# A four-layer gated transformer on one core: the last layer's expert blocks scatter with addition into the output tensor instead of an internal one

## The chip, the cores and the metric

The kernel runs on one NeuronCore of a Trainium2 chip. The core has five engines with queues of their own: TensorE (PE, with its weight loads listed as PEld), VectorE (DVE), ScalarE (ACT), GpSimd (POOL) and SyncE (SP). Matrix products go to PSUM, everything else lives in SBUF or in HBM. SP and ACT issue plain DMAs; indirect DMAs, whose row numbers come from a table in SBUF, are issued by POOL. All DMAs share 16 DMA engines. The metric is the device time of one execution in microseconds; the median of three runs stands for a kernel, and one further execution was recorded by the hardware profiler.

## The reference

The input x is 4 x 256 tokens of 256 values. Four layers follow, each with a gated cross attention to 64 context tokens and a gated feed-forward part: `x = x + tanh(g) * part(layernorm(x))`. The feed-forward parts are a mixture of 16 experts with 6 chosen for each token (layer 0), a ternary-weight network (layer 1), an int8 linear map (layer 2), and again a mixture of experts (layer 3), the one that matters here, cut to its core:

```python
shared_out = silu_and_mul(x @ shared_gate_up) @ shared_down
probs = softmax(x @ gate_w)
topk_w, topk_i = lax.top_k(probs, K)              # K = 2 of E = 8 experts
topk_w = topk_w / sum(topk_w)
combine = sum(one_hot(topk_i, E) * topk_w[..., None], axis=1)
for e in range(E):
    moe_out += combine[:, e, None] * (silu_and_mul(x @ w_gate_up[e]) @ w_down[e])
return moe_out + shared_out
```

Its result, times the gate and added to x, is the kernel's output, 1024 rows of 256 float32 values, 1 KB each.

## The kernel before

**Tiling.** x is held in SBUF as eight tiles of 128 tokens. Layer 3's feed-forward part is `ffn3` (L1425). It normalises the tokens, stores them with their expert weights in an internal HBM tensor `xd`, and works out the routing; beside this it computes the shared expert tile by tile and adds it to x. `keep_rows` (L369) then stores the eight tiles of x in the internal HBM tensor `sums3` from SP's queue (L372), each as soon as its tile of x is finished. What is left is to add the routed experts' results to those rows.

**Blocks.** The routing sorts the 2048 pairs of token and expert into blocks of 128 slots, each block of one expert. An expert's last block is padded. For every slot there are two tables in SBUF, `gather` and `scatter`, made in `placed` (L1133 to L1138). A padding slot of partition p has the scatter index 1024 + p, so the padding rows of a block land in 128 spare rows at the end of `sums3`, which therefore has T + P = 1152 rows. In the same way layer 0's two tensors `sums0` have spare rows. `prepare` (L303) sets the spare rows of all three tensors to zero early in the kernel, with DMAs of 128 KB from a tile of zeros through `zeroed` (L361, issued at L362).

**The loop over blocks.** `Experts` (L1168) serves layers 0 and 3. For block i, `fetch` (L1183) gathers 128 rows of `xd` with an indirect DMA on POOL, four blocks ahead. `turn` (L1194) transposes them on PE, `up` (L1218) multiplies with the expert's two up matrices in SBUF and applies silu (L1246) and the product with the weight (L1247), `turn_hidden` (L1249) transposes the result, and `down` (L1258) multiplies with the down matrix and copies the product to a slot of a ring of eight (on DVE, L1271, for odd blocks, on ACT, L1273, for even ones). Last, `down` issues the scatter (L1274): an indirect DMA on POOL that adds the 128 rows of the ring's slot to the rows of `sums` that the scatter table names. Two blocks can hold the same token, so each scatter waits on POOL's queue until the one before it on the same tensor has landed. Layer 3 has one such tensor, layer 0 two in turn.

**What is sure to run.** In layer 3 the first 20 blocks (`SURE3`) always run; three more stand behind `tc.If` (L1286), under a test of how many blocks are in use. With the reference's inputs the eight experts get 238, 522, 384, 159, 181, 179, 130 and 255 rows, which make just 20 blocks and leave 512 padding slots in them.

**The end.** After the last step four DMAs copy 256 rows each from `sums3` to the output tensor `out`, HBM to HBM, two from SP and two from ACT (L1670 to L1674). They wait for the last scatter to land. Then comes the closing block, whose instructions the profile puts at L1808: SP passes a row of waits for everything outstanding, each engine drains, and all five meet twice at semaphores, with POOL as the one that collects and releases.

**Order.** Instructions of an engine stand in the order in which the framework's scheduler put them; waits between engines and for DMAs are semaphores that the framework derives from reads and writes of tiles and HBM tensors.

Of the kernel before, what the change touches and what calls it, by code (L numbers as in the profile page):

```python
# [29 lines left out]
F32 = mybir.dt.float32  # L30
# [8 lines left out]
P = 128  # L39
B, S, D = 4, 256, 256  # L40
T = B * S
# [41 lines left out]
def tile_flamingo(ctx: ExitStack, tc: tile.TileContext, a: dict, out: bass.AP):  # L83
    nc = tc.nc
# [3 lines left out]
    dram = ctx.enter_context(tc.tile_pool(name="dram", bufs=1, space=bass.MemoryType.DRAM))  # L88
    psum = ctx.enter_context(tc.tile_pool(name="psum", bufs=2, space=bass.MemoryType.PSUM))

    def ps_mm():
        return psum.tile([P, 512], F32, tag="mm", name="mm", bufs=4)
# [4 lines left out]
    def t4(shape, name, dtype=F32):  # L97
        return sb.tile(shape, dtype, tag="t4", name=name, bufs=6)
# [4 lines left out]
    class Carver:  # L103


        def __init__(self, *regions):
            self.left = list(regions)
# [195 lines left out]
    def prepare():  # L303


        work = t4([P, 1024], "work")
        bd_v = work[:, : B * P].rearrange("p (b l) -> p b l", b=B)
        rot = work[:, B * P : B * (P + DC)].rearrange("p (b d) -> p b d", b=B)
        nc.gpsimd.memset(bd_v, 0.0)
        hd = DC // 2  # L310
        cos_k = ropek[:, 0:1, :].to_broadcast([P, B, DC])
        nc.vector.tensor_tensor(kvr, ctx2, cos_k, ALU.mult)
        for lo, hi in ((0, hd), (hd, 0)):
            sin_k = ropek[:, 1:2, lo : lo + hd].to_broadcast([P, B, hd])
            nc.vector.tensor_tensor(rot[:, :, lo : lo + hd], ctx2[:, :, hi : hi + hd], sin_k, ALU.mult)
        nc.vector.tensor_tensor(kvr, kvr, rot, ALU.add)
        yield
        for j in range(2):
            rows = slice(j * L, (j + 1) * L)
            nc.vector.tensor_copy(bd_v[rows, :, j * DC : (j + 1) * DC], kvr[rows])  # L320
        yield
        ps = ps_mm()
        for b in range(B):
            nc.tensor.transpose(ps[:, b * P : (b + 1) * P], bd_v[:, b, :], ident)
        nc.scalar.copy(bd_k.rearrange("p b l -> p (b l)"), ps)
        yield

        ps = ps_mm()
        for b in range(B):
            nc.tensor.transpose(ps[:DC, b * P : (b + 1) * P], ctx2[:, b, :], ident)  # L330
        nc.scalar.copy(ctxT.rearrange("d b j l -> d (b j l)"), ps[:DC, :])
        yield

        bias_t = sb.tile([P, 512], F32, tag="low", name="bias_t", bufs=1)[:96, : 2 * F0]
        nc.sync.dma_start(out=bias_t, in_=a["L0_b13"])
        nc.vector.tensor_copy(causal16, causal)
        nc.vector.tensor_copy(ident16, ident)
        nc.vector.tensor_copy(shared_is, shared_32)
        nc.vector.memset(ones16, 1.0)
        yield  # L340
        yield
        yield
        nc.vector.tensor_copy(bias_0, bias_t)
        for rows in (slice(32, 64), slice(64, 96), slice(64, 96)):

            nc.vector.tensor_tensor(bias_t[rows], bias_t[rows], bias_0[rows], ALU.subtract)
            nc.vector.tensor_copy(bias_0[rows], bias_t[rows])
            yield
        zeros = t4([P, 1024], "zeros")
        nc.gpsimd.memset(zeros, 0.0)  # L350
        for half in range(2):
            zeroed(sums0[1][half * TH : (half + 1) * TH], zeros)
        for sums in (*sums0, *sums3):
            zeroed(sums[T:], zeros)
        yield


    sums0 = [dram.tile([T + P, D], F32, tag=f"sums0{i}", name=f"sums0{i}") for i in range(2)]
    sums3 = [dram.tile([T + P, D], F32, tag="sums3", name="sums3")]

    def zeroed(rows, zeros):  # L361
        nc.sync.dma_start(out=rows.rearrange("(p r) d -> p (r d)", p=P), in_=zeros[:, : rows.shape[0] * D // P])  # L362
# [299 lines left out]
    def attention0(gate):  # L662
# [76 lines left out]

        wide = None  # L740
        later = prepare()
        last: list = []
        output = fold_output(w_kv0, [lambda: (w_o0, NH, lambda: None)])
# [424 lines left out]
    class Experts:  # L1168


        def __init__(self, route, xd, n, nb, stride, width, chunk, sums, w, bias, hTs, between):
            self.gather, self.scatter, self.expert, self.offset, self.used = route
            self.xd, self.experts, self.nb, self.stride = xd, n, nb, stride
            self.width, self.chunk, self.n = width, chunk, width // chunk
            self.sums, self.w, self.bias, self.hTs = sums, w, bias, hTs
            self.between = between
            self.ring = [sb.tile([P, 4, D], F32, tag="xT", name="ring", bufs=2) for _ in range(2)]
            self.weight: dict = {}
            self.xs: dict = {}
            self.at: dict = {}  # L1180
            self.st: dict = {}
# [76 lines left out]
        def down(self, b):  # L1258
            (st, hT), r = self.st.pop(b), self.at.pop(b) + 4 * self.width
            ps = ps_mm()  # L1260
            for j in range(self.n):
                nc.tensor.matmul(  # L1262
                    ps[:, :D],
                    hT[:, j * P : (j + 1) * P],
                    self.w[: self.chunk, bass.ds(r + j * D, D)],
                    start=(j == 0),
                    stop=(j == self.n - 1),
                )
            y = self.ring[b // 4 % 2][:, b % 4, :]
            if b % 2:  # L1270
                nc.vector.tensor_copy(y, ps[:, :D])  # L1271
            else:
                nc.scalar.copy(y, ps[:, :D])  # L1273
            nc.gpsimd.indirect_dma_start(  # L1274
                out=self.sums[b % len(self.sums)],
                out_offset=bass.IndirectOffsetOnAxis(ap=self.scatter[:, b : b + 1].bitcast(U32), axis=0),
                in_=y,
                in_offset=None,
                compute_op=ALU.add,
            )  # L1280

        def run(self, sure):
# [38 lines left out]
    def ffn0(gate):  # L1321
# [45 lines left out]
        def down(t):  # L1367
# [12 lines left out]
            gated_add(t, ps[:, :D], gate)  # L1380

        in_three(NT, up, turn, down)
        for _ in steps:
            pass
# [40 lines left out]
    def ffn3(gate):  # L1425
# [39 lines left out]
        def down(t):  # L1465
# [4 lines left out]
            gated_add(t, ps[:, :D], gate)  # L1470

        in_three(NT, up, turn, down)
        for _ in steps:
            pass
# [55 lines left out]
    def ffn1(gate):  # L1530
# [45 lines left out]
        def down(g, terms):  # L1576
            for i in range(TPG):
# [12 lines left out]
                gated_add(g * TPG + i, y, gate)  # L1590

        in_turn(NG, up, down)
        used("L1_w1")
        used("L1_w2")
# [72 lines left out]
            kept["weights2"] = weights2(tg[:, 6:7])  # L1667
        step(tg[:, k : k + 1])

    for i in range(4):  # L1670
        rows = slice(i * T // 4, (i + 1) * T // 4)
        to, of = (v[rows].rearrange("(p r) d -> p (r d)", r=4) for v in (out, sums3[0]))
        engine = nc.scalar if i % 2 else nc.sync
        engine.dma_start(out=to, in_=of)  # L1674

def _rope(length, dim):
# [133 lines left out]
```

## Time and profile before

| what | value |
|---|---|
| median of three runs | 948.43 us (945.85 to 948.74) |
| the profiled execution: its time | 947.2 us |
| its span, first to last instruction | 945.4 us |
| mean granted TensorE clock | 0.959 |
| PE busy | 844.9 us (89%) |
| DVE, POOL, ACT busy | 514.0, 344.5, 288.7 us |
| layer 3's 20 scatters | 1573 ns each on POOL, 827.1 to 935.2 us |
| layer 3's 20 gathers | 973 ns each on POOL |
| copies to the output | issued 939.0 to 939.7 us |

The time of an execution is a little longer than its span, here by 1.8 us. An engine's busy time counts its instructions' durations; waits, branches and the issue of DMAs on SP and ACT are not in it. [...]"DMA to landing" is the time from the issue to the completion semaphore. In the tables of groups, a line names source line, engine, operation, what is written and read and how often, then busy time and mean duration, then the idle time of the engine just before and what ended most of it. In lists of one tensor's or one line's instructions the three durations are the smallest, the median and the largest, followed by the first and the last start. In the chain of work, each line has a start, a length and an item of the chain.

### The profile page before, as it was taken

The numbers are of one execution on the slowest core, as the hardware profiler recorded it, in microseconds if no ns is written. First come the engines' busy times: TensorE is split into PE (matmuls) and PEld (weight loads), VectorE is DVE, ScalarE is ACT, GpSimd is POOL, SyncE is SP. The second block draws the span as 40 slices with busy tenths as digits, with TensorE's granted clock in tenths as the row PEclk, the third lists the DMA queues.
The fourth block names the chain that finished last, engine by engine and source line by source line (L and its number), as shares of the span: only waits on it lengthen the run. The fifth ranks groups of instructions, "written<-read, shape, count | busy, mean of one in ns | idle before, by whom it ended". The sixth has DMA issues, their size and how long they took to land. (4 is left out here: it accounts for less than half of the span.)

```text
span 945.4 us, 12712 instructions
## 1 busy us (share of the span) xinstructions
PE 844.9 (89%) x4464; PEld 547.3 (58%) x4467; DVE 514.0 (54%) x1299; ACT 288.7 (31%) x561; POOL 344.5 (36%) x262
## 2 busy tenths in 40 slices
PE   5999999999999998899089997899869899999994
PEld 4544335876667875676045873665545556666662
DVE  4666457756934344573146765778777865222220
ACT  2221004433222332233013436516545531122221
POOL 0455452310066777787201232502312402144321
PEclk9999999999999998999589999989989999999997
DMA  9200228101156555654570000180000011122223
GB/s 359 93 16 22 79 65 258 52 18 32 56 158 161 125 121 128 156 86 71 117 266 1 1 1 1 42 302 2 1 23 1 1 47 58 40 47 48 38 23 66
DMA packets 38762, 75.15 MB, mean 79 GB/s; under 512 B 6240, under 2 KB 26706, under 8 KB 37322
## 3 DMA queue, kind: packets, MB, share of 16 engines
q1 hardware_dynamic: 23562, 52.01, 16.4%
q0 software_dynamic: 14496, 20.47, 12.9%
q10 hardware_dynamic: 640, 1.84, 0.5%
q8 instruction: 39, 0.64, 0.3%
q14 instruction: 25, 0.20, 0.1%
HBM read 58.73 MB, written 16.61 MB: 80 GB/s over the span
## 5 line engine op out<-in xcount | busy, mean ns | idle before, releaser
L438 POOL TENSOR_TENSOR attn<-attn,sm 128x1024 f32<-128x1024 f32 x32 | 60.8, 1901 | 197.1 <-DVE sm L437 163.9
L1247 DVE SCALAR_TENSOR_TENSOR blk<-wide,weight,blk 128x176 f32<-128x176 f32 (+1 forms) x75 | 37.0, 494 | 138.0 <-ACT blk L1246 137.9
L1274 POOL DMA_INDIRECT sums<-ring,big x55 | 87.5, 1590 | 34.9 <-issue 10.8
L422 PE MATMUL wide<-xT,big 128*128 128x512 f32 x192 | 88.3, 610 | 0.3 <-ACT big L557 0.3
L684 DVE TENSOR_TENSOR rope<-wide,big 128x512 f32<-128x512 f32 x96 | 59.6, 684 | 48.8 <-PE wide L422 47.5
L1227 PE MATMUL wide<-big,blk 128*128 x220 | 77.0, 472 | 0.1
L1186 POOL DMA_INDIRECT xs<-xd,big x55 | 55.1, 1001 | 55.8 <-DMA sums<-x 35.6
L1238 PE MATMUL wide<-big,blk 128*128 x160 | 72.2, 593 | 0.5 <-DVE blk L1199 0.5
L1246 ACT ACTIVATE blk<-wide 128x176 f32<-128x176 f32 (+1 forms) x75 | 29.4, 392 | 122.5 <-PE wide L1238 60.2
L422 PEld LDWEIGHTS wide<-xT,big 128*128 128x128 f32 x192 | 35.8, 193 | 47.6 <-issue 41.3
L657 PE MATMUL mm<-vo,attnT 128*128 128x256 f32 x256 | 58.6, 382 | 0.9 <-ACT attnT L453 0.9
L1262 PE MATMUL mm<-big,blk 88*128 x220 | 57.6, 384 | 0.5 <-ACT blk L1255 0.5
L407 PE MATMUL mm<-ident,xn 128*128 128x128 f32 x112 | 19.9, 322 | 41.5 <-DVE xn L395 35.4
L657 PEld LDWEIGHTS mm<-vo,attnT 128*128 128x128 f32 x256 | 47.4, 190 | 8.7 <-ACT attnT L453 2.9
L453 ACT COPY attnT<-mm 128x512 f32<-128x512 f32 x64 | 34.6, 589 | 54.7 <-PE mm L452 54.2
L1262 PEld LDWEIGHTS mm<-big,blk 88*128 88x128 f32 x220 | 42.0, 192 | 16.0 <-ACT blk L1255 1.4
L1227 PEld LDWEIGHTS wide<-big,blk 128*128 128x128 f32 x220 | 40.7, 196 | 13.3 <-issue 1.2
L436 DVE TENSOR_REDUCE sm<-attn 128x16 f32<-128x1024 f32 x32 | 38.8, 1213 | 16.3 <-ACT attn L430 13.7
L1186 POOL DMA_INDIRECT xs<-xd,scratch x20 | 19.5, 973 | 76.2 <-PE mm L1198 54.0
L1274 POOL DMA_INDIRECT sums<-ring,scratch x20 | 31.5, 1573 | 39.2 <-ACT ring L1273 16.8
L1238 PEld LDWEIGHTS wide<-big,blk 128*128 128x128 f32 x160 | 28.8, 190 | 28.9 <-issue 28.2
L407 PEld LDWEIGHTS mm<-ident,xn 128*128 128x128 f32 x112 | 15.1, 162 | 47.2 <-ACT rstd L383 27.6
(321 smaller groups left out, 1704.3 us busy)
## 6 DMA issues: line engine op xcount, KB each, us to landing
big<-in_L_w_gate_up SPq DMA_DIRECT2D x8, 1024.0 KB, 8.2
big<-in_L_w SPq DMA_DIRECT2D x4, 1408.0 KB, 7.9
big<-in_L_w_down SPq DMA_DIRECT2D x8, 512.0 KB, 9.3
w_L_qk<-in_L_qk SPq DMA_DIRECT2D x4, 896.0 KB, 8.7
big<-in_L_w SPq DMA_DIRECT2D x4, 704.0 KB
big<-in_L_wo SPq DMA_DIRECT2D x1, 2048.0 KB, 12.9
xd<-xn SPq DMA_DIRECT2D x16, 128.0 KB, 1.8
sums<-x SPq DMA_DIRECT2D x16, 128.0 KB, 1.8
```

Source lines behind the costliest of these rows:

```text
L407: nc.tensor.transpose(ps[:, i * P : (i + 1) * P], n[:, c * P : (c + 1) * P], ident)
L422: nc.tensor.matmul(ps, w(c), xT[:, c, :], start=(c == 0), stop=(c == 1))
L436: nc.vector.tensor_reduce(sm, e, AX.X, ALU.add)
L438: nc.gpsimd.tensor_tensor(e, e, sm.unsqueeze(2).to_broadcast([P, groups, n]), ALU.mult)
L657: nc.tensor.matmul(ps[:, :D], aT[:, s, :], vo[:, s, :], start=(s == 0), stop=(s == NP - 1))
L684: nc.vector.tensor_tensor(m[:, s, :].rearrange("q (b t) -> q b t", t=S), ps[:, s, :].rearrange("q (b t) -> q b t", t=S), table, ALU.mult,)
L1186: nc.gpsimd.indirect_dma_start(out=xs, out_offset=None, in_=self.xd, in_offset=bass.IndirectOffsetOnAxis(ap=self.gather[:, b : b + 1].bitc ...
L1227: nc.tensor.matmul(ps[:, 0, : 2 * n], st[:, c * P : (c + 1) * P], self.w[:, bass.ds(r + c * 2 * n, 2 * n)], start=False, stop=(c == 1),)
L1238: nc.tensor.matmul(ps[:, k, :n], st[:, c * P : (c + 1) * P], self.w[:, bass.ds(r + (2 * c + k) * n, n)], start=(c == 0), stop=(c == 1),)
L1247: nc.vector.scalar_tensor_tensor(s, lin, self.weight.pop(b), s, ALU.mult, ALU.mult)
L1262: nc.tensor.matmul(ps[:, :D], hT[:, j * P : (j + 1) * P], self.w[: self.chunk, bass.ds(r + j * D, D)], start=(j == 0), stop=(j == self.n - 1),
L1274: nc.gpsimd.indirect_dma_start(out=self.sums[b % len(self.sums)], out_offset=bass.IndirectOffsetOnAxis(ap=self.scatter[:, b : b + 1].bitca ...
```

## The change

Layer 3's sum tensor is now the output tensor itself, so `keep_rows` stores layer 3's x there and the scatters add to it. The output has 1024 rows and no spare ones. The scatters of layer 3 therefore carry a bound, 1023: a row whose index is greater is out of bounds, and that is declared not to be an error. Layer 0's tensors have 1152 rows, so its scatters keep having no bound. The spare rows of layer 3's tensor no longer exist and aren't set to zero. The four copies at the end are gone.

```diff
-        for sums in (*sums0, *sums3):
+        for sums in sums0:
             zeroed(sums[T:], zeros)
         yield
...
     sums0 = [dram.tile([T + P, D], F32, tag=f"sums0{i}", name=f"sums0{i}") for i in range(2)]
-    sums3 = [dram.tile([T + P, D], F32, tag="sums3", name="sums3")]
+    sums3 = [out]
...
             self.between = between
+            rows = sums[0].shape[0]
+            self.bound = rows - 1 if rows == T else None
...
                 in_offset=None,
                 compute_op=ALU.add,
+                bounds_check=self.bound,
+                oob_is_err=self.bound is None,
             )
...
-    for i in range(4):
-        rows = slice(i * T // 4, (i + 1) * T // 4)
-        to, of = (v[rows].rearrange("(p r) d -> p (r d)", r=4) for v in (out, sums3[0]))
-        engine = nc.scalar if i % 2 else nc.sync
-        engine.dma_start(out=to, in_=of)
```

## The prediction

> **What bounds the kernel now.** I read the page's slices first, for where TensorE is the limit and where it is not.
>
> ```profile
> span 945.4 us, 12712 instructions
> PE   5999999999999998899089997899869899999994
> DMA  9200228101156555654570000180000011122223
> ```
>
> Each digit is a fortieth of the span, 23.6 us. TensorE is busy nine tenths nearly everywhere, layer 3's expert blocks included (the last five slices), and only the last slice falls to 4: the tail is where something else sets the end. The table by stage shows both:
>
> ```profile
> 827.00:931.00 104.00, 103.33 (x390) 64.50 (x388) 26.69 (x71) 24.66 (x45) 38.42 (x29) 1.00 0.26 38
> 939.00:945.40 6.40, 0.00 (x0) 0.00 (x0) 0.00 (x0) 0.00 (x0) 0.00 (x0) 0.50 0.48 165
> ```
>
> The columns are length, then busy time (and count) of PE, PE's weight loads, DVE, ACT, POOL. From the first scatter to the last up-projections PE works 103.33 of 104 us; in the last 6.4 us no engine works at all. What is between them, from the chain that ended last:
>
> ```profile
> 928.17 1.74 PE mm L1262 x8
> ...
> 930.76 3.72 DMA sums<-ring,scratch
> ...
> 935.32 1.44 POOL sums L1274
> ```
>
> Block 18's scatter is issued at 930.76 and lands 3.72 us later; only then may block 19's go (935.21, its data had been ready since 933.51). After it come the four copies to the output:
>
> ```profile
> L1674 SPq DMA_DIRECT2D out_dram<-sums x2: 529/548/567, 939.0 to 939.7; - x2
> L1674 ACTq DMA_DIRECT2D out_dram<-sums x2: 598/686/775, 939.0 to 939.7; - x2
> DMA to landing us min/median/max: 3.9/4.2/4.4
> ```
>
> They start at 939.02, so the last scatter landed about 938.96 (935.21 + 3.75). The last two are issued at 939.7 and land 4.4 us or a little more later, about 944.3. Last I asked for the closing block (L1808), where every engine meets:
>
> ```profile
> L1808 SPq EVENT_SEMAPHORE  x14: 17/28/28, 940.3 to 945.3; - x14
> L1808 POOLq EVENT_SEMAPHORE  x4: 17/17/17, 944.6 to 945.3; - x4
> L1808 POOLq DRAIN  x3: 50/109/4327, 936.6 to 945.1; - x3
> ```
>
> SP first passes twelve waits here, then all engines meet at POOL's event of 944.6; from there to the end are 0.8 us. The third line matters: POOL's first drain starts at 936.57 and lasts 4.33 us, to 940.90, which is 1.94 us after the last scatter's landing. Today it is hidden under the copies.
>
> **Part 1, the closing copies go.** Today: landing 938.96, copies until 944.3, closing to 945.4. Without them two paths lead to the meeting point:
> - SP: landing 938.96; its remaining waits are already satisfied and pass at 62 ns each (eight of them between 940.27 and 940.70), at most twelve, so 0.7 us: 939.7.
> - POOL: the drain, to 940.90.
> The later one decides. From the drain: 940.90 + 0.8 = 941.7 us of span, 3.7 us saved. From SP alone: 939.7 + 0.1 + 0.8 = 940.6, 4.8 us saved. Here a rule stands against the row. The Trainium skill, "VectorE: DVE Perf Modes", section "The DRAIN you can't avoid", says that the drains of a kernel's start and end are boilerplate of about 12 ns on all five engines. By it POOL's drain would be free and the saving 4.8 us; by the row it is 4.33 us long. The row decides here: SP's drains do last 7 ns, but this one stands behind a scatter in flight, and it still does after the change. I take 3.7 and keep 4.8 as the other end: if the drain waits for the copies rather than for the scatter, it shrinks.
>
> A second rule bears on the size. "DMA: Bandwidth & Descriptors", "Anatomy of one DMA", puts a software-issued DMA at 2.0 us plus bytes over 436 GB/s. For 1 MB in all that estimates 4.4 us from first issue to last landing; the trace has 5.3 (939.02 to 944.3). By the rule 0.9 us less would be removed; the measured copies decide.
>
> **Part 2, the bound on each scatter.** No row has a bounded scatter. The nearest are the unbounded one and the gather:
>
> ```profile
> L1186 POOL DMA_INDIRECT xs<-xd,scratch x20 | 19.5, 973 | 76.2 <-PE mm L1198 54.0
> L1274 POOL DMA_INDIRECT sums<-ring,scratch x20 | 31.5, 1573 | 39.2 <-ACT ring L1273 16.8
> ```
>
> Call d the extra time from issue to landing of one bounded scatter (a register with 1023, a comparison for each of 128 indices). Upper end: the 0.60 us (1.573 - 0.973) that separates scatter from gather, the price of a further treatment of each row. Lower end: below zero only where rows are skipped. With the reference's inputs all 20 blocks are in use (the experts get 238, 522, 384, 159, 181, 179, 130 and 255 rows), 512 of 2560 slots are padding, but block 18 has none and block 19 one; the tail gains nothing from skipping, 0. I take d = 0.15, nearer the unbounded row since that already reads the same 128 indices. What it costs: in the loop nothing, for the period is PE's 5.82 us (905.15 to 910.97 between activations), and scatter to scatter needs 3.75 to land plus 0.48 until the next is issued, 4.23; there is 1.6 us of cover. POOL's own queue holds 0.98 of gather and 1.57 of scatter per period, so a gather queued behind is not late either, and four blocks are prefetched. In the tail the cover is gone: block 19's scatter waits for block 18's, so d counts twice, 0.3 us (0 to 1.2).
>
> **Part 3, the target is the output tensor.** Eight stores of layer 3's rows move from the internal tensor to the output, the same SP issues:
>
> ```profile
> L372 SPq DMA_DIRECT2D sums<-x x5: 319/320/320, 799.8 to 814.9; - x5
> ```
>
> The last goes at 814.9, and with 1.8 us to land is there by 816.7, 10 us ahead of the first scatter (827.1); even one waiting for another's landing, 1.8 us against 5.6 us between them, would be hidden. Each scatter keeps waiting for its predecessor, since both add to the same rows. Cost 0; were a store or scatter to the output tensor slower by some tenths, it would enter like d.
>
> **Part 4, one zeroing fewer** (L362, five issues of about 0.46 us, at 107.0 to 109.9): SP's queue is 700 us ahead of the tail there, and PE's slice at 107 us is full. 0, at most 0.5 us gained.
>
> **Sum.** 3.7 - 0.3 = 3.4 us: span 945.4 to 942.0, the profiled execution 947.2 (1.8 around the span) to 943.8. That execution lies 1.2 us below the median of the runs, 948.43; carried over, **945.0 us**.
>
> **The rivals.**
> 1. SP ends the kernel, the drain shrinks: 4.8 - 0.3 = 4.5 saved, 943.9. For it: SP's 7 ns drains. Against: the row of 4.33 us.
> 2. The bound eats the gain: d of 0.4 to 1.2 in the tail twice, or a slower landing in the output, leaves 3.7 - 0.8 to 3.7 - 2.4, so 2.9 to 1.3 saved: about 946.3, no measurable change. For it: the 0.60 us between gather and scatter. Against: the padding rows are data, not another instruction.
> 3. Slower: scatter and landing of the bounded form take so long that they set layer 3's pace. The point from which it decides is d = 1.6 us, where the 1.6 of cover is spent and 3.7 - 3.2 = 0.5 is left of the gain; from there each further 0.1 us costs 19 x 0.1 in the loop and 0.2 in the tail, so at 1.63 the gain is gone. At d = 2, a serial treatment of skipped rows, the last scatter is issued at 827.1 + 19 x 6.23 = 945.5 and lands at 951.2; drain 1.94 and closing 0.8 make 954.0, +8.6: 957. For it: nothing in the trace bounds a skipping accumulate. Against: it must more than double a 1.57 us instruction.
> 4. The change does nothing: if the wait for the output's own writes took as long as the copies. Against: scatters land in 3.75 us already[...]. 948.4.
>
> **Chances.** The forecast 0.48, rival 1 0.16, rival 2 0.17, rival 3 0.14, rival 4 0.05. Under 0.3% (2.8 us) a measurement of this kernel can hardly tell a change from none: the three runs spread over 2.9 us. The forecast lies only 0.6 us beyond that, so of its share 0.05 falls to "same", and 0.02 of rival 2 to "faster": faster 0.61, same 0.25, slower 0.14. The range runs from rival 1 with 1.2 us of the spread of runs (942.7) to rival 2's poorer end with as little above it (947.8), and leaves rival 3 and half of rival 4 out.
>
> **What the profile after would show.** No L1674; last scatter issued near 935.4; POOL's long L1808 drain still about 4.3 us, ending near 941.2, and the meeting event right behind it, span near 942. A drain under 1 us means rival 1. The bounded scatters' row against 1573 ns and their landing against 3.8 show d; packets on the software queue fall by 512 if padding is skipped. "POOL sums <- DMA sums" waits in many places instead of one, with PE waiting for nothing new, mean rival 3. The prediction is wrong if d exceeds 0.6, or if the last scatter's landing in the output is slower than in the internal tensor.

## The result and the profile after

The changed kernel takes 945.6 us (median of 22 runs) against 948.59 us for the kernel before (22 runs on the same chip). The ratio is 0.9971 with a 95% interval from 0.9957 to 0.9985: 2.8 us less, between 1.4 and 4.1. The forecast was 945.0 us. The profiled execution took 945.0 us with a span of 942.8 us, against 947.2 and 945.4 before.

The output tensor's own instructions in the profile after (name, smallest, median and largest duration in ns, first and last start; below, what POOL's idle time in front of a scatter ended with):

```profile
L1276 POOL DMA_INDIRECT out_dram<-ring,scratch x20: 1552/1574/1638, 828.1 to 936.4; - x20
L372 SPq DMA_DIRECT2D out_dram<-x x8: 332/332/342, 783.1 to 815.8; - x8
...
  DMA out_dram<-ring,scratch: 3.1, 1
```

The 20 scatters cost POOL 1574 ns each, as the unbounded ones did (1573). One of them, as before, waits for the landing of its predecessor: the last. The stores are in place 10 us ahead of the first scatter. The closing copies' line is absent.

The end of the chain of work (start, length, item):

```profile
931.69 3.94 DMA out_dram<-ring,scratch
...
936.50 1.44 POOL out_dram L1276
```

Block 18's scatter goes at 931.69 and lands after 3.94 us, then block 19's goes at 936.39; its semaphore is complete at 940.02. Then the closing block, now at L1806:

```profile
L1806 SPq EVENT_SEMAPHORE  x14: 17/28/28, 937.7 to 942.7; - x14
L1806 POOLq EVENT_SEMAPHORE  x4: 17/17/17, 942.0 to 942.7; - x4
L1806 POOLq DRAIN  x3: 50/109/4210, 937.7 to 942.5; - x3
```

POOL's first drain starts at 937.74, lasts 4.21 us and ends at 941.95; the engines meet at POOL's event of 942.0 and 0.8 us later the kernel ends. SP was through with its waits at 940.65 and stood still for 1.3 us. The drain that was hidden under the copies is what ends the kernel now.

For comparing traces I use the stretch from the first scatter of layer 3 to the end of the span. The scatters and the copies lie in it; the stores of x and the zeroing, which the change also touches, lie ahead of it. It was 118.26 us before (827.14 to 945.40) and is 114.71 us after (828.08 to 942.79): 3.55 us less. The span gained less, 2.6 us, since the first scatter came 0.94 us later in this execution. The time gained less again, 2.2 us: the part of it that lies outside the span is 2.2 us here, where it was 1.8.

### The profile page after: what moved, and what is told of

Its sections match the earlier page's. It is cut to its first block, busy times and chain, and to the rows that moved or that the text cites. A ratio compares the mean times of both kernels' runs of the same rounds, so it can differ in the third digit from the quotient of the medians.

```text
span 942.8 us, 12721 instructions
## 1 busy us (share of the span) xinstructions
PE 845.5 (90%) x4464; PEld 547.2 (58%) x4467; DVE 513.2 (54%) x1299; ACT 288.5 (31%) x561; POOL 344.9 (37%) x262
## 5 line engine op out<-in xcount | busy, mean ns | idle before, releaser
L1276 POOL DMA_INDIRECT out_dram<-ring,scratch x20 | 31.5, 1574 | 39.4 <-ACT ring L1275 16.8
L457 DVE SCALAR_TENSOR_TENSOR x<-mm,tg,x 128x256 f32<-128x256 f32 x48 | 23.0, 478 | 35.4 <-PE mm L657 16.2
```

The costliest lines, as they stand in the source:

```text
L1276: nc.gpsimd.indirect_dma_start(out=self.sums[b % len(self.sums)], out_offset=bass.IndirectOffsetOnAxis(ap=self.scatter[:, b : b + 1].bitca ...
```

## The experiments

Each trace gives the stretch and the end of POOL's first closing drain, counted from the last scatter's landing; the times are ratios to the kernel before on the same chip. The ratio of the kernel with a second scatter rests on two runs, those of "POOL works later still" and "an early drain" on three each.

| kernel | stretch, us | drain's end after last landing, us | ratio of times (95%) |
|---|---|---|---|
| before | 118.26 | 1.93 | |
| after | 114.71 | 1.93 | 0.9971 (0.9957 to 0.9985) |
| after, again | 114.79 | 1.93 | 0.9974 (0.9957 to 0.9991) |
| copies left out | 114.77 | 1.93 | 0.9965 (0.9949 to 0.9981) |
| bound alone | 118.09 | 1.93 | 1.0015 (1.0000 to 1.0031) |
| POOL works later | 118.04 | 5.29 | 0.9980 (0.9961 to 0.9999) |
| second, skipped scatter | 155.52 | 5.35 | 1.0432 (1.0275 to 1.0590) |
| half the copies | 117.44 | 1.93 | 1.0006 (0.9987 to 1.0024) |
| POOL works later still | 121.39 | 8.48 | 1.0053 (1.0020 to 1.0086) |
| last scatter left out | 110.01 | 1.89 | 0.9911 (0.9893 to 0.9928) |
| no conditional part | 114.65 | 1.93 | 0.9956 (0.9923 to 0.9988) |
| an early drain | 114.27 | 1.68 | 0.9954 (0.9930 to 0.9978) |

**The changed kernel again.** No edit.

> The changed kernel as it is, a second time, to separate what belongs to the change from what one execution does. In its first profile the tail gained 3.6 us (from the first layer-3 scatter to the end 114.71 us against 118.26 before), but the first scatter came 0.93 us later (828.08 against 827.14), and that shift stands already at 18 us of the span. Theory: the shift is how one execution starts and no part of the change; here the stretch from first scatter to end is again 114.7 +/- 0.3 us, while the start of the first scatter lies anywhere from 826 to 829. Rival: the change moves something early in the kernel, and the first scatter is again at 828.1 or later, 0.9 us after that of kernels with the old early part. Time against the kernel before: 3.0 us less.

The stretch repeats to 0.1 us (114.79). The first scatter came at 830.29, later than the 826 to 829 expected, and by itself that would fit the rival. But in later kernels with the same early part it came at 827.23 (POOL works later) and 825.48 (second scatter), and at 829.40 and 829.74 in two more; in three with the old early part it came at 827.14 to 827.78 (two profiles with a slower layer 0, further down, are left aside). So the start of the first scatter varies by almost 5 us with one and the same early part, and the 0.94 us between the first two profiles needs no cause in the change. That the change moves the early part by some tenths is not excluded. The time repeats as well.

**The copies alone.** The kernel before without its last loop; the output is not written.

```diff
-    for i in range(4):
-        rows = slice(i * T // 4, (i + 1) * T // 4)
-        to, of = (v[rows].rearrange("(p r) d -> p (r d)", r=4) for v in (out, sums3[0]))
-        engine = nc.scalar if i % 2 else nc.sync
-        engine.dma_start(out=to, in_=of)
```

> The kernel before with its four closing copies left out and nothing else changed: internal sum tensor with spare rows, no bound. The output is not written. Theory (the copies are all of the gain, the bound and the output as target are free): first scatter to end 114.7 us as in the changed kernel, 3.0 to 3.6 us less time than before, POOL's closing drain some 4.2 us long and ending 1.93 us after the last scatter's landing. Rival (the bound or the new target also costs or gains something): a difference of more than 0.5 us to the changed kernel in the stretch from first scatter to end.

114.77 us: the copies are all of the gain in the stretch, to 0.1 us, with the internal tensor as target and without a bound. POOL's drain is the same:

```profile
L1802 POOLq DRAIN  x3: 50/109/4330, 937.3 to 942.2; - x3
```

**The bound alone.** In the kernel before:

```diff
                 compute_op=ALU.add,
+                bounds_check=None if self.bias is not None else T - 1,
+                oob_is_err=self.bias is not None,
             )
```

> The kernel before with the bound 1023 on layer 3's scatters alone: internal tensor, zeroed spare rows (now not written by the scatters) and the four copies stay. Theory (the bound costs one register move of 29 ns per scatter, which is hidden, and skipped rows become 8-byte packets): POOL's row 1574 ns per scatter, mean landing 3.67 us instead of 3.79, blocks with about 100 padding rows land near 3.1 us, 512 packets of 8 bytes in place of 512 of 1024; time within 0.5 us of before. Rival (the bound costs 0.15 us or more per scatter, as the forecast assumed): landings of full blocks at 3.95 or more, the last scatter 0.15 and its landing 0.3 us later than before.

POOL's row for these scatters is 1574 ns, the mean landing is 3.66 us against 3.79 before, and blocks 6, 11 and 17 (118, 97 and 126 padding rows) land in 2.98, 3.13 and 2.80 us; in the kernel before they took 3.79, 3.82 and 3.75. The two blocks of the tail, with one padding row between them, land in 3.92 and 3.71 us (before: 3.72 and 3.75). The stretch is 118.09 us, 0.17 less. The packets of the software queue (count, MB, share of 16 engines) show what skipping is:

```profile
q0 software_dynamic: 14496, 19.94, 12.9%
```

The count is the one of the kernel before, the volume 0.53 MB less (20.47): after the first scatter the trace has 2048 packets of 1024 bytes and 512 of 8 bytes, where it had 2560 of 1024. A skipped row stays a packet, of 8 bytes. The time, 1.0015 of before (1.4 us), leans to the slow side with an interval that touches 1; the trace has nothing in the stretch to go with it. The time outside the span is 0.33 us longer than before (2.16 against 1.82 us, means of 14 and 66 runs); the rest stays open.

**What the drain waits for.** Behind the last step of the changed kernel:

```diff
         step(tg[:, k : k + 1])
+
+    back = sb.tile([P, D], F32, tag="xn", name="back", bufs=6)
+    again = sb.tile([P, D], F32, tag="xn", name="again", bufs=6)
+    nc.sync.dma_start(out=back, in_=out[:P])
+    nc.gpsimd.tensor_tensor(again, back, back, ALU.add)
```

> The changed kernel with one thing added behind the last scatter: SP loads 128 rows of the output back to SBUF (so it waits for the last landing), and POOL adds the tile to itself; its result is not used. POOL reaches its closing drain some 3 us later, about 5 us after the last scatter was issued and past the point of 1.93 us after its landing. Theory A (the drain waits for the software DMA, and ends 1.93 us after its landing): the drain is now under 0.3 us long and the span grows by about 1.5 to 2 us. Theory B (a drain behind an indirect DMA takes a fixed 4.2 us from its own start): the drain is again about 4.2 us and the span grows by 4 us or more.

Neither theory holds. The last landing was 939.15, POOL's addition ran from 941.49 to 942.10, and the drain ended at 944.43, 5.29 us behind the landing and 2.34 behind the addition:

```profile
L1811 POOLq DRAIN  x3: 50/109/2979, 941.5 to 945.0; - x3
```

So I added four more such additions (`for _ in range(4): nc.gpsimd.tensor_tensor(again, again, back, ALU.add)`).

> As the kernel in which SP loads 128 rows of the output back and POOL adds them, but with four more such additions behind (0.6 us each): POOL's last instruction ends about 2.4 us later. There the drain started at 941.46, lasted 2.98 us and ended 2.34 us after POOL's addition ended, though the last scatter had landed 5.3 us before; so neither of the two earlier readings held. Theory C (the first drain behind software DMAs does about 2 us of work of its own, beginning when the scatter has landed and POOL has nothing else to do): it ends again about 2.3 us after the last addition, the span grows by 2.4 us more. Theory D (it waits for something that runs beside POOL's additions, such as a fixed delay from SP's load or from the landing): it ends at about the same place after the last scatter's landing, 5.3 us, or with the last addition.

```profile
L1813 POOLq DRAIN  x3: 50/109/3097, 946.8 to 950.5; - x3
```

The last addition ended at 947.61, the drain at 949.95: 2.34 us again, now 8.48 behind the landing. The stretch grew by 3.35 us over the kernel with one addition, not 2.4, since the additions follow each other at 0.80 us and not 0.6. Of the theories so far only C fits both: some 2 us of the drain's own, which begin when POOL is idle and the scatter has landed. What those 2 us are is not shown, and two kernels further down do not fit so small a figure.

**The cover of the scatter chain taken away.** In the changed kernel, behind each scatter of layer 3 a second one of the same slot, with nearly all rows skipped (the token of row 0 is added twice):

```diff
+            if self.bound is not None:
+                nc.gpsimd.indirect_dma_start(
+                    out=self.sums[b % len(self.sums)],
...
+                    compute_op=ALU.add,
+                    bounds_check=0,
+                    oob_is_err=False,
+                )
```

> The changed kernel with a second scatter behind each of layer 3's 20: the same ring slot and indices, but with the bound 0, so that nearly all its rows are skipped (the one token with row 0 is added twice). The scatters of one tensor wait for each other, so this lengthens the chain of scatters by a known amount and takes away the 1.6 us of cover in each block. Theory (a chain of landings, cover gone): a full scatter 3.75 + 0.48 and a skipped one 2.8 + 0.48 (block 17, with 126 skipped rows, landed in 2.8) make a period of 7.5 us instead of PE's 5.82; first scatter to end grows from 114.7 to about 115 + 19 x 1.7 + 3.3 = 150 us, the time by 35 us over the changed kernel. Rival (POOL's scatters are not what sets the pace even then, since they may overlap): growth of the last scatter alone, 3.3 us.

Waits of POOL (who, for what: us in total, times, longest):

```profile
POOL out_dram L1286 <- DMA out_dram<-ring,scratch: 45.3, 19, 3.0
...
POOL out_dram L1276 <- DMA out_dram<-ring,scratch: 15.0, 7, 3.5
```

Where one scatter waited for a landing, 26 do. From the first full scatter (825.48) to the last (968.11) the period is 7.51 us, the expected 7.5, and the time is 1.0432 of before, about 41 us. A skipped scatter lands in 2.7 us, and from a landing to the next issue it is mostly 0.27 us in front of a skipped scatter and 0.76 in front of a full one, where 0.48 was counted for each. So the scatters are a chain that sets layer 3's pace once its cover is used up. The stretch is 5.5 us longer than expected. Some 2 us of that are 19 periods of 1.80 in place of 1.7 us; the other 3.4 are the drain, which ended 5.35 us behind the last landing and 3.97 us behind the instruction with which POOL steps the semaphores of scatters that did not run. Here that instruction ran only after the last landing (975.05 to 976.19, landing at 974.81).

**That instruction as the cause.** The changed kernel without the conditional part of layer 3, which doesn't run with these inputs:

```diff
             self.blocks(0, sure, self.between)
+            if self.bias is None:
+                return
```

> The changed kernel without the conditional part of layer 3 (the three further blocks and their test are left out; with the reference's inputs they don't run). In each run so far POOL passes, behind the last scatter, an instruction that steps the semaphores of the scatters that did not run (0.7 us), and then drains. Theory C (the drain's 1.93 us behind the landing is its own work and follows any scatter): it still ends 1.93 us after the last landing, and first scatter to end stays 114.7 us. Theory E (the delay comes from that stepping of semaphores, since in the kernel with doubled scatters, where it ended 1.4 us after the last landing, the drain ended 5.4 us after the landing): without it the drain ends with the landing, SP's waits decide, and first scatter to end is about 1.2 us less, 113.5.

```profile
L1808 POOLq DRAIN  x3: 50/109/5859, 937.7 to 944.1; - x3
```

The stretch is 114.65 us and the drain ends 1.93 us behind the landing. In the changed kernel, then, the stepping of semaphores is not what makes the drain long. The drain's record is 5.86 us long here, since it begins at 937.68, even before the last scatter's (937.90); its end stays where it was. So its length says little, and the distance from the landing is what repeats. Why the drain took longer in the kernel with doubled scatters stays open.

**Half the copies.** `range(4)` becomes `range(2)` in the last loop of the kernel before; half the output is not written.

> The kernel before with two of its four closing copies (the first 512 rows; the other half of the output is not written). Theory (the copies end the kernel until they land before POOL's drain ends): in the kernel before the first pair landed at 942.9, 1.4 us ahead of the second pair, so first scatter to end is 118.3 - 1.4 = 116.9 us, down to 116 if the second pair slowed the first; still above the 114.8 of no copies, where the drain decides. Rival (the two copies are hidden by the drain): 114.8 us.

117.44 us, 0.8 less than with four, and 2.7 more than with none; 116 to 116.9 were expected. The two copies land at 952.29 at the latest, 3.8 us behind the last scatter; they end the kernel. Alone, the first pair is only 0.15 us earlier behind the last scatter than beside the second pair (3.81 against 3.96 us), which rules out the 116. What lies above 116.9 is behind the copies: from their landing to the end it took 1.66 us instead of 1.06, and why is not shown. The drain, done by 950.41, is hidden:

```profile
L1808 SPq EVENT_SEMAPHORE  x14: 17/28/28, 949.1 to 953.9; - x14
L1808 POOLq EVENT_SEMAPHORE  x4: 17/17/17, 953.1 to 953.8; - x4
L1808 POOLq DRAIN  x3: 50/109/4398, 946.0 to 953.7; - x3
```

The ratio of times, 1.0006 with an interval of 1.8 us to each side, is too coarse to show 0.8 us.

**The last scatter left out.** In the changed kernel block 19's products are not added to the output:

```diff
+            if self.bias is None and b == SURE3 - 1:
+                return
             nc.gpsimd.indirect_dma_start(
```

> The changed kernel without the scatter of block 19 (its 127 rows are not added to the output); its products are still computed. The last scatter is block 18's, issued 103.6 us after the first and landing 3.75 to 3.95 us later. Theory (the end is last landing, plus 1.93 us of POOL's drain, plus 0.84 us of closing): first scatter to end 103.6 + 3.85 + 2.77 = 110.2 us, 4.5 us less than the changed kernel. Rival (the drain has a fixed length of 4.2 us from its own start, or PE's end decides, which comes 105.9 us after the first scatter): more than 111 us, or under 108.

```profile
L1808 POOLq DRAIN  x3: 50/109/4206, 943.9 to 948.6; - x3
```

The stretch is 110.01 us, 0.2 from the expected 110.2: last landing 946.19, 1.89 of drain, 0.84 of closing. Its time is 0.9911 of before, 8.4 us, and the stretches differ by 8.25. In this profile and in that of half the copies the first scatter came some 10 us late. That delay arose ahead of the part that the change touches; the table by stage (length, busy time of PE, PEld, DVE, ACT, POOL, then granted clock, DMA share, GB/s) shows a lower granted TensorE clock in layer 0. First the changed kernel, then this one:

```profile
250.00:275.00 25.00, 21.77 (x105) 14.14 (x104) 13.76 (x67) 3.75 (x10) 9.04 (x10) 0.93 0.51 143
```

```profile
250.00:275.00 25.00, 23.94 (x93) 15.60 (x92) 11.73 (x56) 3.22 (x8) 4.98 (x5) 0.68 0.29 87
```

0.68 against 0.93, and 0.69 in the profile of half the copies. It is a reason to compare stretches and not spans.

**A drain with nothing in flight.** In the changed kernel, before layer 3's blocks, tied to the last instruction of the layer's normalisation:

```diff
+        dr = nc.gpsimd.drain()
+        tc.add_manual_dep(dr.ins, kept["normal"].ins.name, ...)
         moe = Experts(route[0], xd, E3, NB3, W3, F3, P, sums3, big, None, hTs, lambda i: None)
```

> The changed kernel with one more drain of POOL in layer 3, after the layer's normalisation and ahead of its first gather, where no software DMA is in flight. Theory C1 (the drain's own work clears what software DMAs since the last drain have left, so an earlier drain takes a share of it): the early drain lasts about 1 to 2 us, and the closing one ends clearly less than 1.93 us after the last landing. Theory C2 (the work is the same in each drain that follows a software DMA, however many there were): the early one lasts about 2 us, the closing one ends 1.93 us after the landing as before. Theory C3 (only a DMA still in flight makes a drain long): the early one lasts under 0.2 us, the closing one ends 1.93 us after the landing. In each case the time is that of the changed kernel to within 1 us.

```profile
L1487 POOLq DRAIN  x1: 6193/6193/6193, 766.1 to 766.1; - x1
```

```profile
L1813 POOLq DRAIN  x3: 52/103/3821, 938.8 to 943.2; - x3
```

The early drain lasts 6.19 us, though POOL had done nothing for 9 us (its last operation ended at 756.8) and no software DMA was under way. That speaks against C3: a DMA in flight is not needed for a long drain. It is one execution, and the drain's end falls 0.05 us behind the VectorE operation that POOL's next instruction waits for (772.26), so it is not shown that all of the 6.19 us is the drain's own work. The closing drain ends 1.68 us behind the landing, a quarter of a microsecond earlier than in eight other traces, where it was 1.93 or 1.89. That is what C1 says in sign, but in size most of the 1.93 stays, and 6.2 us for 112 software DMAs on POOL before it is out of proportion to 1.7 for the 40 after. What the drain does in that time stays open.

## Why the prediction was right, step by step

- **Part 1, the copies go.** Right in its mechanism: POOL's drain, hidden until then, ends the kernel, and SP waits for it. The 3.7 us read from the drain's row were 0.2 too many. The kernel without copies gives 3.5 us and the changed one 3.55, since the last landing came 0.1 us later in the stretch than before (111.93 us behind the first scatter, against 111.82) and the closing took 0.84 to 0.90 us instead of 0.8. What the forecast could not say, whether the drain hung on the scatter or on the copies, the runs decide: it stands 1.93 us behind the landing without any copy.
- **The two rules.** The rule of 12 ns, read as holding for this drain too, would have given the wrong number: POOL's drain lasted 4.21 us after the change. The Trainium skill, "VectorE: DVE Perf Modes", section "The DRAIN you can't avoid", gives that figure for boilerplate drains of the runtime's preamble and postamble, and this drain stands at a line of the kernel (L1806), so the two need not be the same. The other engines' drains at that line do last only 7 to 17 ns. The second rule, for software-issued DMAs, does not bear on these copies: the trace has them on the queues `q1 hardware_dynamic` and `q10 hardware_dynamic`, 64 packets each. The forecast didn't use it.
- **Part 2, the bound.** Its size was off: d was put at 0.15 us and is nothing that can be measured. POOL's row is 1574 ns against 1573. In seven traces with the bound block 18 lands in 3.86 us and block 19 in 3.73 on average; in three without it (before, copies left out, half the copies) in 3.79 and 3.77. The sum of the two differs by 0.03 us where 0.3 was counted. The register move of 29 ns fits into the time between the ring's copy and the issue, 0.46 us in both kernels. That the loop pays nothing was right, with the reason given: the doubled scatters show the chain of landings at 7.51 us a period once the cover is gone. The cover itself was counted too large. From block 18's landing to block 19's issue it took 0.73 us before and 0.76 after, not 0.48, which makes it about 1.2 to 1.3 us instead of 1.6 (an estimate: a period of 5.76 us less 3.79 to land and 0.73 to 0.76).
- **Part 3, the output as target.** 0 for the scatters, as counted: the internal tensor and the output give the same stretch (114.77 and 114.71). One reading was wrong. The last five stores are 5.6, 5.6, 2.2 and 1.7 us apart, so 5.6 us does not hold between all of them; the 10 us ahead of the first scatter are what hides them.
- **Part 4, a zeroing fewer.** It lies ahead of the stretch, where starts vary by almost 5 us from one execution to the next. Neither the 0 nor the 0.5 us allowed for could be seen.
- **The sum.** 3.4 us was forecast and 3.55 measured in the stretch. That the two lie so near is in part luck: 0.2 us too much for the copies and 0.3 too much for the bound nearly cancel. In the profiled span 0.94 us of the gain was missing, through an execution that reached layer 3 later. The 1.8 us around the span, which the forecast carried over, became 2.17 on average in both measurements of the changed kernel (22 runs each; before: 1.82 in 66), so some 0.35 us of the gain is lost outside the span. The bound alone shows it too (2.16), the copies left out don't (1.80); but two kernels with the bound have 1.83, so its cause stays open. The ratios of the two measurements, 2.8 and 2.5 us, hold 3.5 us in their intervals. The upper end of the range, 947.8, is 0.5 below what its own words give (947.1 and 1.2 more); the measured time is far from either.
- **The rivals.** SP's path does not end the kernel (rival 1): it waits 1.3 us for POOL. The bound does not eat the gain (rival 2), nor set the pace (rival 3). The mechanism of rival 3 is real, as the doubled scatters show; from which d on it would decide was not measured. Rival 4 falls with the copies left out.
- **The signs to look for.** The drain ended at 941.95 where 941.2 was expected, 0.94 of it the late start. One sign was wrong: the packets of the software queue do not fall by 512, only their bytes do.

## What to carry to other kernels

A copy at the very end, with no engine working beside it, is worth its full length less whatever it was hiding: list what each engine does in the closing block, its drains too, before counting on the saving. A scatter with addition can go straight to the output, since a bound takes the place of spare rows at no cost that the traces here show, as long as each scatter still waits for the one before (no run here left that wait out). Executions that differ by a microsecond in parts that were not changed are compared by the stretch that holds the change, and the median over many runs still decides what the change is worth.

## What the runs showed of the hardware

- A drain of POOL behind indirect DMAs is not short. It ended 1.93 us after the last landing in seven of the ten traces in which POOL computed nothing behind the scatters, and 1.89, 1.68 (after an early drain) and 5.35 us (doubled scatters) in the other three. Where POOL did compute, it ended 2.34 us after its last addition, twice. In the middle of the kernel, with no software DMA in flight, one lasted 6.19 us. The two closing drains that follow last 0.1 and 0.05 us.
- A row that the bound skips is still a packet on the software queue, of 8 bytes instead of 1024. A scatter of 128 rows lands in about 3.8 us; one with 97 to 126 skipped rows in 2.8 to 3.2, with one exception of 3.74 (block 17 in the kernel without the conditional part); and one with all or nearly all rows skipped in 2.7.
- POOL's time for a scatter does not depend on skipping: its row is 1573 ns without and 1574 with a bound, and 1552 ns at the least in both.
